# First chunk's values and third unit's queries and keys as seven block products

## The chip, the cores and the metric

The kernel runs on one core of a Trainium2 chip. The core has five engines with a queue of instructions each: TensorE (PE in the profile, with its weight loads as PEld), VectorE (DVE), ScalarE (ACT), GpSimd (POOL) and SyncE (SP), which here only issues DMAs. The time is the device time of one execution in microseconds; the time before is the median of three runs.

## The reference

One layer: a layer norm, causal attention with 32 heads of 16, and a gate, over x of shape 2 x 1024 x 512 in float32.

```python
xn = _layernorm(x, axis=-1)
s = _L0_attn_ref(xn, Wq, bq, Wk, bk, Wv, bv, Wo, bo)       # causal, 32 heads of 16
g = _silu(_L0_ffn_ref(xn, W_base, b_base, W_gate, A, B))   # 8 experts of rank 16, top 2
x = x + s * g
```

Inside the attention, q, k and v are xn @ W.T + b. The scores are q . k / 4 under a causal mask, then softmax, then the sum over v, then the output projection.

## The kernel before

**Work and stages.** Each batch (2) is cut into two chunks of 512 tokens, and the 512 columns of queries and keys into four groups `oc` of 8 heads. A *unit* (b, oc, c) is the attention of one chunk's queries for one group. The units run in the order of `units` (lines 1305 to 1311): the first is (0, 0, 0), the second (0, 1, 0), the third (0, 0, 1), which is the second chunk of the first group. A unit is a list of *steps*. `plan` strings the steps of all units together (144), and the loop at the end of `direct` does for each step n: `scores(n)` (PE into two PSUM tiles, then two exponentials on ScalarE), `values(n - 1)` (PE, the weights of the step before times the values), `masked(n)` (GpSimd clears what lies above the diagonal), and `fill(n)`, which puts other work in. The first unit has steps 0 to 4, the second 5 to 9, the third 10 to 22.

**Who sets the order.** The whole program is written down in one pass, and each engine takes its instructions in that order. `fill` (line 1513) is a planner: a `Task` is a generator with a due step, a cost in PE time (`MM` = 0.853) and conditions. It takes PE tasks until the step's share is spent, and then lets through what waits in the list `later`: small pieces for the other engines, each with the step from which it may go. A piece with an entry in `costs` goes when ScalarE is reckoned calm, and at the latest at its second number. `Metered` and `Queue` keep the planner's reckoned times of VectorE, ScalarE and SP.

**Buffers.** Projections write PSUM tiles of the tag `mm`, of which there are two, so a product can only begin when the product before the last one has been read. Scores have two tiles a step (`ps_s`, two of each name), so scores n + 1 can begin when the exponentials of step n have read theirs. The exponentials' results `pt` have three buffers.

**Products by blocks.** Most projections are made by a scheme in which a 2 x 2 block matrix product takes seven block products instead of eight: `four_sums` makes four sums t1 to t4 of weight blocks, `sums_task` four sums s0 to s3 of token blocks, and the products p1, p2, p6, p7, p5, p3, p4 (for queries and keys q1 to q4, with the query's and the key's columns as the two block columns) are added up on VectorE. Value and gate products are `block_task`, those of queries and keys `qk_blocks_task`. Weight sums are stored to DRAM (`kept`) and loaded again piece by piece into four buffers with the tag `wp` (`issue_parts`). Three projections are made in the plain way: the first unit's queries and keys (`first_task`), the second and third unit's (`qk_task`), and the first chunk's values (`v_task`, one of four token tiles at a time, each 4 groups of four matmuls).

**Rounding.** From the second unit on, keys and queries are split into a high part in fp32r and a remainder. `split_keys` rounds the keys on ScalarE (`kT<-kf`) and takes the remainder on VectorE; `split_queries` and `copy_remainder` do so for queries; `place_keys` and `place_queries` put the remainders onto other partitions, by two DMAs each on SP's queue. The first unit uses unrounded keys `kf_0_0_0`; they are also the first keys of the third unit, so they are shuffled, rounded and placed later (`apart` in `first_task`). `pair_up` is a copy on ScalarE that rearranges a weight tile's columns before a block product or `qk_task` can use it.

Almost all vector and scalar instructions are recorded at line 56 and all SP DMAs at line 72, so the profile's groups are told apart by their tiles.

Of the kernel before, what the change touches and what calls it, by code (L numbers as in the profile page):

```python
# [18 lines left out]
P = 128  # L19
D = 512  # L20
# [77 lines left out]
def direct(ctx, tc, sound, x, wq, wk, wv, wo, wb, wa, wg, wB, bq, bk, bv, bo, bb, out):  # L98
# [259 lines left out]
    def first_task():  # L358
# [78 lines left out]
        later.append((0, lambda: pair_up(wqks[1])))  # L437
        paired = lambda: pair_up(wqks[0])
        costs[paired], costs[apart] = (1.1, 5), (1.1, 6)
        later.append((3, paired))  # L440
        later.append((4, apart))
        yield 2 * MM
# [117 lines left out]

    first_v = []

    def v_task(b, i):
        if not first_v:
            first_v.append(value_tile(b, 0))
        pv = mm_tile("pv")
        for _ in project(pv, b, i, wv_sb):
            yield MM
        ve.tensor_add(
            heads(first_v[0])[:, i, :, 0:HD],  # L570
            pv.rearrange("p (h r) -> p h r", h=H),
            bv_sb.rearrange("p (h r) -> p h r", h=H),
        )
        vs[b, i] = first_v[0][:, i]
        yield MM

# [4 lines left out]
    groups = (  # L584
        [("v", 0, 1), ("qk", 0, 1, 1)],
        [("gate", 0, 0), ("qk", 0, 0, 2), ("qk", 0, 0, 3)],
# [29 lines left out]

    def combine_task(name, given=None):

        src, bias = weights[name]
        w = given or load_whole(src, f"w_{name}", later)  # L620
        for _ in range(0 if given else 6):
            yield WAIT
        at = {
            (i, j): w[:, 2 * i : 2 * i + 2, BK * j : BK * j + BK]
            for i in range(2) for j in range(2)
        }
        yield from four_sums(at, {int(t[1]): at[p] for t, p in IN_PLACE.items()})
        kept = dram.tile([P, KC, D], F32, tag=f"kept_{name}", bufs=1, name="kept")
        ve.tensor_tensor(bias[:, BK:D], bias[:, BK:D], bias[:, 0:BK], ALU.subtract)
        yield WAIT  # L630
        combined[name] = kept
        if given:
            sp.dma_start(out=kept, in_=w)
            kept_at[name], kept_lands[name] = now[0], sp.landing()
        if name == "gate":
            first = stages.index(("gate", 0, 0))
            for j, part in enumerate(PARTS):
                if part in IN_PLACE:
                    places[first, j] = at[IN_PLACE[part]]
                    held.add((first, j))  # L640
        for kc in range(0 if given else KC):
            yield WAIT
            sp.dma_start(out=kept[:, kc], in_=w[:, kc])
            kept_at[name], kept_lands[name] = now[0] + KC - 1 - kc, sp.landing()
        yield WAIT
        if given:
            yield WAIT
        while name == "gate" and made[first] < len(PARTS):
            yield WAIT

    def issue_parts():
        while issued[0] < len(parts):
            k, j = parts[issued[0]]
# [22 lines left out]
            issued[0] += 1  # L676

    def qk_weights_task(n):

# [4 lines left out]
        else:  # L684
            if n >= 2:
                wqks.append(load_qk(oc))
                for _ in range(3):
                    yield WAIT
                paired = lambda: pair_up(wqks[n])
                costs[paired] = (1.05, now[0] + 4)  # L690
                later.append((now[0] + 1, paired))
                while any(x[1] is paired for x in later):
                    yield WAIT
                yield WAIT
            w = wqks[n]
            yield from four_sums(
                {(i, j): w[:, 4 * j + 2 * i : 4 * j + 2 * i + 2] for i in range(2) for j in range(2)},
                {t: w[:, 2 * KC + 2 * t - 2 : 2 * KC + 2 * t] for t in range(1, 5)},
            )
            qk_kept[oc] = dram.tile([P, 4 * KC, P], F32, tag=f"kept_qk{oc}", bufs=1, name="kept")  # L700
            qk_ready[n] = now[0]
            for i in range(4):
# [127 lines left out]

    def qk_blocks_task(k):

        _, b, c, oc = stages[k]
        at, w = tokens(k), wqks[b * KC + oc]
        qk_begun.append((b, oc, c))
# [3 lines left out]
        less, bias = b_less[:, oc : oc + 1], b_pair[:, KC + oc : KC + oc + 1]  # L839
        place = {"11": 0, "21": 2, "12": 4, "22": 6, "t1": 8, "t2": 10, "t3": 12, "t4": 14}  # L840

        def product(name, a):
            ps = mm_tile(name)[:, 0:BK]
            n = place[PARTS[made[k]]]
            for kc in range(2):
                matmul(ps, lhsT=w[:, n + kc], rhs=a[:, kc], start=kc == 0, stop=kc == 1)
            made[k] += 1
            return ps
# [8 lines left out]
        yield MM  # L857
        s = yield from sums_of(k)
        add(keys[0], product("q6", s[1]), keys[0])
# [6 lines left out]
        yield MM  # L866
        add(keys[0], product("q3", s[3]), keys[0])
        yield MM
        add(q[1], product("q4", at(1, 1)), q[1], less)
        splits.append((now[0] + 1, lambda: split(b, oc, c, qf, kf), (b, oc, c)))  # L870
        qk_done[b, oc, c] = now[0]
        ended[0] += 1
        yield MM

    def values_task(k):
# [511 lines left out]
    for b in range(NB):  # L1387
        for c in range(NC):
# [11 lines left out]
            for oc in range(KC):  # L1400
                takes = {"acc": 1}
                if (b, oc, c) in units[1:3]:
                    Task(
                        starts[b, oc, c] - (1 if c else 2), qk_task(b, oc, c), 8 * MM, takes=takes | {"qT": 1, "kT": 1}, uses=xn, frees=takes,
                        ready=lambda u=units[units.index((b, oc, c)) - 1], t=turned_: u in qk_begun
                        and t() and (u == units[0] or now[0] >= starts[units[1]]),
                    )
                elif oc or b or c:
                    stage(
# [3 lines left out]
            if not b and not c:  # L1413
                room["v"] -= 1
                for t in range(TT):
                    Task(
                        s0 + (1, 2.9, 5, 2.9)[t], v_task(b, t), 4 * MM, uses=xn + [("xnT", "wv")],
                        ready=turned_,
                    )
                Task(  # L1420
                    3, combine_task("v", wv_sb), 0.0, after=5, uses=[("xnT", "wv")],
                )
                for n, name in enumerate(("gate", "out")):
                    Task(
                        (20, 48)[n], combine_task(name), 0.0, after=(9, 34)[n], takes={"xnT": 1},
                        frees={"xnT": 1}, ready=lambda n=n: len(combined) > n,
                    )
                for n in range(2 * KC):
                    Task(
                        (20, 13, 24, 28)[n] if n < KC else -9, qk_weights_task(n), 0.0, after=9,  # L1430
                        ready=lambda n=n: n < 2 or (
# [771 lines left out]
```

## Time and profile before

| what | us |
|---|---|
| median of three runs | 548.98 (548.91 to 549.15) |
| the profiled execution, its own time | 548.63 |
| its span, first to last instruction | 546.8 |
| PE busy in the span | 536.9 |
| DVE, ACT, POOL busy | 333.0, 351.7, 117.9 |
| first value product begins | 17.64 |
| scores of step 10 begin (third unit) | 67.76 |

Times in a timeline are microseconds from the span's start, followed by the length; `xN` is the number of instructions in a piece, and a bracket says how long the engine sat idle before it and what ended that. A float32 matmul leaves two records. `pv` are the first chunk's values, `pq` and `pk` queries and keys made in the plain way, `p` and `q` block products, `ph` the routing's logits, `s` scores, `av` values times weights. The ends of matmuls are modelled, so a busy PE may hold short waits.

### The profile page before, as it was taken

How to read it: one execution, taken by the hardware profiler on the slowest of the kernel's cores; microseconds unless marked ns; L12 is line 12 of the kernel's file. 1: busy time of each engine (PE TensorE's matmuls, PEld its weight loads, DVE VectorE, ACT ScalarE, POOL GpSimd, SP SyncE). 2: the span in 40 equal slices, each digit the busy share in tenths (PEclk: the TensorE clock that was granted, in tenths of full speed). 3: DMA queues.
4: the chain of work that ended last, by engine and by line, in shares of the span. 5: the costliest groups of instructions: out<-in, count | busy, mean ns of one | idle time of the engine just before them, and what ended most of it. 6: DMA issues, size and time to landing. Idle time of an engine off the chain costs nothing.

```text
span 546.8 us, 19460 instructions
## 1 busy us (share of the span) xinstructions
PE 536.9 (98%) x8411; PEld 278.3 (51%) x8411; DVE 333.0 (61%) x692; ACT 351.7 (64%) x390; POOL 117.9 (22%) x249
## 2 busy tenths in 40 slices
PE   8999999999999999999999999999999999999994
PEld 8435444554455544454645554454545554455562
DVE  4435586665575975576379766575176553648842
ACT  2437754776776867657667756657668767777531
POOL 2213401020134411030123321130123331020500
PEclk9999999999999999999999999999999999999999
DMA  8734357356527376813646545640123221652301
GB/s 262 183 101 159 133 161 233 99 177 197 175 99 230 120 243 209 220 42 100 199 153 197 187 131 176 198 137 23 64 99 123 86 75 46 232 172 86 99 22 66
DMA packets 66798, 78.11 MB, mean 143 GB/s; under 512 B 9880, under 2 KB 51872, under 8 KB 66064
## 3 DMA queue, kind: packets, MB, share of 16 engines
q1 hardware_dynamic: 66688, 76.78, 44.1%
q8 instruction: 68, 1.11, 0.8%
q14 instruction: 26, 0.21, 0.1%
q10 hardware_dynamic: 16, 0.00, 0.0%
HBM read 45.34 MB, written 19.37 MB: 118 GB/s over the span
## 4 chain that ended last, share of the span: by engine, by line
PE 95%; DVE 2%; ACT 1%; issue 0%; POOL 0%; ACTq 0%; POOLq 0%; DVEq 0%
PE av L1676 26%; PE p L257 23%; PE s L1624 18%; PE q L257 14%; PE ph L257 3%; PE pv L257 3%; PE po L257 2%; PE pk L257 1%; PE pq L257 1%; ACT pt L56 1%; PE warm L212 1%; PE pq_first L385 1%; PE h L257 1%; DVE g L56 1%; PE pk_first L385 1%
## 5 line engine op out<-in xcount | busy, mean ns | idle before, releaser
L56 ACT ACTIVATE pt<-s 128x1024 f32<-128x1024 f32 x288 | 290.4, 1025 | 151.8 <-PE s L1624 144.8
L1652 POOL TENSOR_SCALAR_AFFINE_SELECT pt<-pt 128x256 f32<-128x256 f32 (+1 forms) x224 | 108.6, 501 | 405.4 <-ACT pt L56 404.8
L1676 PE MATMUL av<-pt,v 128*32 128x512 f32 (+3 forms) x1680 | 155.7, 467 | 0.4 <-DVE v L56 0.2
L1624 PE MATMUL s<-qT,kT 32*128 32x512 f32 (+3 forms) x1616 | 108.2, 363 | 0.7 <-ACT pt L56 0.5
L1624 PEld LDWEIGHTS s<-qT,kT 32*128 32x128 f32 x1616 | 62.0, 183 | 59.4 <-issue 34.9
L1676 PEld LDWEIGHTS av<-pt,v 128*32 128x32 f32 x1680 | 41.1, 108 | 54.6 <-issue 38.8
L257 PE MATMUL p<-wt,asum 128*32 128x256 f32 x864 | 52.6, 379 | 0.0
L257 PE MATMUL q<-asum,wqk 128*32 128x256 f32 x832 | 51.1, 379 | 0.0
L257 PEld LDWEIGHTS p<-wt,asum 128*32 128x32 f32 x864 | 28.5, 110 | 26.4 <-issue 11.2
L257 PE MATMUL q<-xnT,wqk 128*32 128x256 f32 x624 | 39.5, 379 | 0.0
L257 PEld LDWEIGHTS q<-asum,wqk 128*32 128x32 f32 x832 | 26.8, 110 | 23.7 <-issue 7.2
L56 DVE TENSOR_TENSOR g<-p,g 128x512 f32<-128x512 f32 x20 | 13.8, 690 | 26.6 <-PE p L257 26.5
L257 PEld LDWEIGHTS q<-xnT,wqk 128*32 128x32 f32 x624 | 20.2, 110 | 18.5 <-issue 6.6
L56 DVE SCALAR_TENSOR_TENSOR kf<-q,kf 128x256 f32<-128x256 f32 x39 | 16.5, 424 | 21.3 <-PE q L257 20.6
L257 PE MATMUL p<-w,xnT 128*32 128x256 f32 x448 | 27.4, 379 | 0.0
L257 PE MATMUL p<-w,asum 128*32 128x256 f32 x320 | 20.8, 379 | 0.0
L257 PEld LDWEIGHTS p<-w,xnT 128*32 128x32 f32 x448 | 14.9, 110 | 10.6 <-issue 3.3
L257 PEld LDWEIGHTS ph<-wag_sb,xnT 128*32 128x32 f32 x512 | 15.3, 110 | 3.9 <-issue 3.0
L257 PE MATMUL ph<-wag_sb,xnT 128*32 128x136 f32 x512 | 16.6, 279 | 0.0
L56 DVE TENSOR_TENSOR x<-p,x 128x512 f32<-128x512 f32 x15 | 10.3, 688 | 10.3 <-PE p L257 10.2
L257 PE MATMUL po<-wo,oT 128*32 128x512 f32 x128 | 16.5, 592 | 0.0
L56 DVE TENSOR_TENSOR qT<-qf,qT 128x512 fp32r<-128x512 f32 x15 | 10.4, 696 | 9.4 <-ACT qT L56 9.4
(150 smaller groups left out, 565.8 us busy)
## 6 DMA issues: line engine op xcount, KB each, us to landing
wt<-kept SPq DMA_DIRECT2D x36, 256.0 KB
qT<-qT SPq DMA_DIRECT2D x30, 256.0 KB
x<-in_x_dram SPq DMA_DIRECT2D x16, 256.0 KB
kept<-wqk SPq DMA_DIRECT2D x16, 256.0 KB
wqk<-kept SPq DMA_DIRECT2D x4, 1024.0 KB
kT<-kf SPq DMA_DIRECT2D x30, 128.0 KB
scr<-sq SPq DMA_DIRECT2D x6, 512.0 KB
xnT<-scr SPq DMA_DIRECT2D x24, 128.0 KB
```

What stands on the lines that cost most here:

```text
L56: return getattr(self.engine, name)(*args, **named)
L212: nc.tensor.matmul(warm[:, n % 4 * P : n % 4 * P + P], lhsT=ident, rhs=ident, start=True, stop=True)
L257: nc.tensor.matmul(o[j : j + 32], lhsT=lhsT[:, j : j + 32] if len(lhsT.shape) == 2 else lhsT[:, j // 32], rhs=rhs, start=start, stop=stop,)
L385: nc.tensor.matmul(ps[:, cols], lhsT=w[:, k, :], rhs=xnT[:, k, cols], start=k == 0, stop=k == KC - 1)
L1624: nc.tensor.matmul(ss[s // 2][:, s % 2, col : col + w], lhsT=keys[rows, kt % TT * P : kt % TT * P + P], rhs=q[rows, halves * par + half_, ...
L1652: nc.gpsimd.affine_select(out=d, in_=d, compare_op=ALU.is_ge, fill=0.0, base=0, pattern=[[0, d.shape[1]], [1, P]], channel_multiplier=-1,)
L1676: nc.tensor.matmul(avs_now[par][32 * s : 32 * s + 32, q0 : q0 + w], lhsT=vs[b, kt][:, h * VS - HD * par : h * VS - HD * par + HP], rhs=pt[ ...
```

## The change

1. The first chunk's values are made by `early_task` as seven block products instead of four plain tiles. It makes its eight sums itself, on VectorE: six before the first product's addition, two before the second's. Its products are written in the order p1, p2, p6, p7, p4, p5, p3, with each addition written right behind its product. The weight sums lie in the four `wp` buffers and not in place, and `keep_task` stores them to DRAM by four DMAs; the products of the second chunk's values can be loaded only after that.
2. The third unit's queries and keys become a block stage: seven products of two groups of four matmuls at 256 columns. Their token sums s0 to s3 are shared with the second chunk's values. In this unit the keys are rounded right behind the product q3, and the queries behind q4, instead of by the planner's `splits`.
3. For that, the first weights' pairing copy (`paired`) is offered at step 1 and the weight sums of the first group follow at step 3.
4. The first unit's keys (`apart`) are offered at step 7 instead of 4, and at the latest at 8 instead of 6.
5. Due steps of some tasks change (second unit's `qk_task` 3, gate weights 18).

The diff, cut to its core:

```diff
@@ first_task
-        paired = lambda: pair_up(wqks[0])
-        costs[paired], costs[apart] = (1.1, 5), (1.1, 6)
-        later.append((3, paired))
-        later.append((4, apart))
+        def paired():
+            pair_up(wqks[0])
+            paired_at.append(now[0])
+
+        costs[paired], costs[apart] = (1.1, 4), (1.1, 8)
+        later.append((1, paired))
+        later.append((7, apart))
...
-        [("v", 0, 1), ("qk", 0, 1, 1)],
+        [("qk", 0, 1, 0), ("v", 0, 1), ("qk", 0, 1, 1)],
...
+    def keep_task():
+        kept = dram.tile([P, KC, D], F32, tag="kept_v", bufs=1, name="kept")
+        for part, (r, o) in IN_PLACE.items():
+            sp.dma_start(
+                out=kept[:, 2 * r : 2 * r + 2, BK * o : BK * o + BK], in_=early_sums[part]
+            )
+            if part in ("t3", "t2"):
+                yield WAIT
+        combined["v"], kept_at["v"], kept_lands["v"] = kept, now[0], sp.landing()
...
@@ qk_blocks (was qk_blocks_task)
+        soon = (b, oc, c) == units[2]
...
         add(keys[0], product("q3", s[3]), keys[0])
+        if soon:
+            qT, kT = split_tiles(b, oc, c)
+            split_keys(kT, kf, kf)
+            later.append((now[0], lambda: place_keys(kT, kf)))
         yield MM
         add(q[1], product("q4", at(1, 1)), q[1], less)
-        splits.append((now[0] + 1, lambda: split(b, oc, c, qf, kf), (b, oc, c)))
+        if soon:
+            split_queries(qT, qf)
+
+            def remainder():
+                copy_remainder(qT)
+                urgent.append((now[0], lambda: place_queries(qT)))
+
+            later.append((now[0] + 1, remainder))
+            room["acc"] += 1
+        else:
+            splits.append((now[0] + 1, lambda: split(b, oc, c, qf, kf), (b, oc, c)))
...
+    def early_task():
+        x0 = xnTs[0, 0]
+        at = lambda i, j: x0[:, 2 * j : 2 * j + 2, BK * i : BK * i + BK]
+        raw = {
+            (i, j): wv_sb[:, 2 * i : 2 * i + 2, BK * j : BK * j + BK]
+            for i in range(2) for j in range(2)
+        }
...
+        def product(name, a, w):
+            ps = mm_tile(name)
+            for i in range(2):
+                for kc in range(2):
+                    matmul(
+                        ps[:, i * BK : i * BK + BK],
+                        lhsT=a[:, kc, i * P : i * P + P],
+                        rhs=w[:, kc],
+                        start=i + kc == 0,
+                        stop=i + kc == 2,
+                    )
+                    yield MM / 2
+            return ps
+
+        sub = lambda o, a, b: ve.tensor_tensor(o, a, b, ALU.subtract)
+        sub(t[1], raw[0, 1], raw[0, 0])
+        sub(s[2], at(0, 0), at(1, 0))
+        sub(s[1], at(1, 1), s[2])
+        sub(t[2], raw[1, 1], t[1])
+        ve.tensor_tensor(s[0], s[1], at(0, 0), ALU.add)
+        sub(t[3], raw[1, 1], raw[0, 1])
+        p1 = yield from product("p1", at(0, 0), raw[0, 0])
+        add(s12, p1, bias(0))
+        sub(t[4], raw[1, 0], t[2])
+        sub(s[3], at(0, 1), s[1])
+        p2 = yield from product("p2", at(0, 1), raw[1, 0])
+        add(s11, p2, s12)
+        begin_with[0].due = 2
+        sub(bv_sb[:, BK:D], bv_sb[:, BK:D], bv_sb[:, 0:BK])
+        p6 = yield from product("p6", s[1], t[2])
+        add(s12, p6, s12)
+        p7 = yield from product("p7", s[2], t[3])
+        add(s21, p7, s12)
+        ve.tensor_tensor(s22, s21, bias(1), ALU.add)
+        p4 = yield from product("p4", at(1, 1), t[4])
+        add(s21, p4, s21)
+        begin_with[0].due = 3
+        p5 = yield from product("p5", s[0], t[1])
+        add(s12, p5, s12)
+        add(s22, p5, s22)
+        ve.tensor_tensor(s12, s12, bias(1), ALU.add)
+        p3 = yield from product("p3", s[3], raw[1, 1])
+        add(s12, p3, s12)
...
-                if (b, oc, c) in units[1:3]:
+                if (b, oc, c) == units[1]:
+                    begin_with.append(Task(
+                        1, early_task(), 14 * MM, takes={"v": 1},
+                        uses=xn + [("xnT", "wv")], ready=turned_,
+                    ))
                     Task(
-                        starts[b, oc, c] - (1 if c else 2), qk_task(b, oc, c), 8 * MM, takes=takes | {"qT": 1, "kT": 1}, uses=xn, frees=takes,
...
+                        3, qk_task(b, oc, c), 8 * MM, takes=takes | {"qT": 1, "kT": 1}, uses=xn, frees=takes,
                     )
+                elif (b, oc, c) == units[2]:
+                    stage(
+                        qk_blocks_task, ("qk", b, c, oc), starts[b, oc, c] - 2, 7 * MM,
+                        takes | {"qT": 1, "kT": 1}, xn,
+                        lambda t=turned_: t() and begin_with[0] not in tasks,
+                    )
+                    summed[0].due = 4
...
-                for t in range(TT):
-                    Task(
-                        s0 + (1, 2.9, 5, 2.9)[t], v_task(b, t), 4 * MM, uses=xn + [("xnT", "wv")],
-                        ready=turned_,
-                    )
-                Task(
-                    3, combine_task("v", wv_sb), 0.0, after=5, uses=[("xnT", "wv")],
-                )
+                Task(4, keep_task(), 0.0, after=4, ready=lambda: begin_with[0] not in tasks)
```

## The prediction

> **What bounds the kernel now.** I read the page first, then the chain of work that ended last piece by piece over the first 120 us, then the instructions in order of time on every engine, and last the order in which the changed program's instructions stand on each engine. The page's busy times, then its chain:
>
> ```profile
> PE 536.9 (98%) x8411; PEld 278.3 (51%) x8411; DVE 333.0 (61%) x692; ACT 351.7 (64%) x390; POOL 117.9 (22%) x249
> ...
> PE 95%; DVE 2%; ACT 1%; issue 0%; POOL 0%; ACTq 0%; POOLq 0%; DVEq 0%
> ```
>
> PE sets the time: PE work removed is time won, and every wait of PE is time lost unless a later wait gets shorter. The chain around the change (start us, length, what; a matmul leaves two records):
>
> ```profile
> 27.14 5.15 PE pv L257 x48
> 32.29 3.43 PE pq L257 x32
> 35.73 3.43 PE pk L257 x32
> 39.16 1.08 PE s L1624 x16
> 40.24 1.00 PE av L1676 x16
> ...
> 46.82 0.70 DVE v L56
> 47.52 0.14 issue
> 47.66 1.07 PE av L1676 x16
> ...
> 66.10 1.73 PE p L257 x32
> ...
> 71.22 0.67 PE s L1624 x5
> ```
>
> The reader is to see that pieces follow each other without a gap, except for the last value tile (46.82 to 47.66). A group of four strips costs 3.43/4 = 0.858 us at 512 columns and 1.73/4 = 0.43 at 256. A plan step outside its filler costs scores 1.08 (first unit) or 0.67 to 0.73, plus av 1.00. I number steps by their scores; step 10 is the third unit's first (scores at 67.83 now).
>
> Durations that the sums below use, from the timeline:
>
> ```profile
> 25.28 0.17 DVE L56 TENSOR_SCALAR rstd<-mv 128x4 f32<-128x4 f32 x1
> 39.95 1.06 ACT L56 ACTIVATE kT<-kf 128x1024 fp32r<-128x1024 f32 x1
> 41.04 0.69 DVE L56 TENSOR_TENSOR kf<-kf,kT 128x512 f32<-128x512 f32 x1 [2.75 <-ACT kT L56]
> 52.77 0.76 DVE L56 STREAM_SHUFFLE low<-kf 128x512 f32<-128x512 f32 x1
> 61.01 1.92 ACT L56 ACTIVATE pt<-s 128x1024 f32<-128x1024 f32 x2
> 62.82 0.63 ACT L56 ACTIVATE qT<-qT 128x512 fp32r<-128x512 f32 x1
> 63.47 1.11 SPq L72 DMA_DIRECT2D qT<-qT  x2
> 68.39 0.54 SPq L72 DMA_DIRECT2D wt<-kept  x1
> 90.89 0.42 DVE L56 SCALAR_TENSOR_TENSOR kf<-q,kf 128x256 f32<-128x256 f32 x1 [0.38 <-PE q L257]
> ```
>
> **Which part can differ.** From step 22 on, PE's instructions stand in the same order in both programs, apart from four matmuls moved by one step near the end (steps 137 and 138). So the difference is what PE gains or loses up to step 22, carried to the end. I walk PE from 17.71, where values begin in both.
>
> **Removed.** Values: 4 x 4 groups of 0.858 = 13.7 become 7 x 4 of 0.43 = 12.1: -1.6. Third unit: 8 groups, 6.9, become 14 of 0.43, 6.1: -0.8. The gap at 46.82 goes, but scores of 0.67 stood inside it: -0.2. Together -2.6. The copy that pairs the first weights (1.15 on ScalarE) moves from step 4 to step 1, where ScalarE is idle from 24.5 to 26.2: nothing. The routing's logits move to steps 3 to 5, at the same PE cost. Two value-weight loads leave SP's queue at step 1, four 256 KB stores enter at step 5 behind the second transposed half; nothing waits for them before step 8. If that cover went, their 4 x 0.5 us of issue would delay the products of step 8.
>
> **Added, steps 0 to 3: VectorE.** It is free at 15.54, and the value weights have landed (the DMA that waits for their semaphore issues at 13.62). In front of the first product's addition stand six 128x512 sums. Such sums take 0.69 (0.77 and 0.89 where GpSimd works beside them); I take 0.72, as the four weight sums at 49.56 take 2.95 together. So 15.54 + 4.3 = 19.9; p1's addition to 20.55; t4 and s3 to 22.0; p2's addition to 22.7. PE: p1 to 19.4, p2 21.15, a quarter of p6 21.6, scores 22.65, av 23.7 (0.05 behind p2's addition), rest of p6 25.0, p7 26.7. Then p4 needs p6's PSUM buffer (two buffers), and in front of p6's addition stand 0.4 for the bias and next chunk's statistics, 21.96 to 25.45 now = 3.5: 22.7 + 0.4 + 3.5 + 0.7 = 27.35. **Stall 0.65.** Likewise pq needs p5's buffer; normalizing (2.1) and transposes (1.4) stand in front of p5's two additions: 29.8 + 3.5 + 1.4 = 34.8 against 34.6. **Stall 0.2.** pk ends 41.65. All sums at 0.69 halve these 0.9; at 0.85 they are 2.
>
> **Steps 3 to 6: ScalarE.** Steps 3 to 5 get shorter (1.08 + 1.00 + 6 x 0.23 = 3.5; step 5 only 0.67 + 1.00 + 0.93 = 2.6), while ScalarE does kf 0.69, kT 1.06 and 2.0 of exponentials after pk, and a 0.27 copy per logits tile. Exponential 3 ends at 45.4, scores 4 wants its buffers at 45.1 to 45.2; scores 6 waits for exponential 5. **Stalls 0.35 and 0.25.** Step 7 begins at 55.2. The second transposed half, now about 2.5 later than its last issue end of 48.8 and landing some 1.6 after it, is there at 52.9, before q2 at 54.3.
>
> **Step 7: five q products in a row.** VectorE: q2's addition to 55.65, four token sums of 0.69 to 58.4, two routing operations to 58.85, only then q6's addition (59.3). q6 waits 0.15 for its sum; q5 needs q6's buffer: 0.55; q4 0.05. **Stall 0.75.** q3 ends at 61.1, q4 at 62.0; q3's addition ends at 61.55.
>
> **Steps 8 and 9: who is queued behind whom.** In the built order ScalarE has kT, qT and the routing exponential in front of exponential 8, and VectorE has the remainder of the keys (which waits for kT) in front of q4's addition (which qT waits for). So after 61.55: kT 1.06, remainder 0.69, q4's addition 0.42, qT 1.06, routing 0.22, with 0.05 each between: exponential 8 runs from 65.2 to 67.2, though its scores are there at 62.75. Now no such pair stands there with a VectorE round trip inside it. PE does av 7 and the value product p1 until 65.5; scores 9 need both buffers of exponential 8: done at 67.85 where 66.15 was possible. av 8 waits for its masks, 0.84 later: **stall 1.7 + 0.2.** p2 ends at 70.8.
>
> **Step 10: the first unit's keys.** They are rounded only now. VectorE: query remainder to 65.7, six small routing operations (1.3 alone, 1.9 beside GpSimd as at 67.03: 1.6), p1's addition 0.68, shuffle 0.76: 68.75. ScalarE: rounding 1.06, query copy 0.63: 70.5. SP's queue: two query placements 1.1 and a weight load 0.54, then the first half of the keys is issued at 72.2. Now that placement (issued 67.19) finds the DMA engines busy from 68.2 to 69.4 for its two halves, so the first lands about 1.6 after issue: 73.8. Scores 10 need it; PE comes at 70.8: **stall 3.05** (landing 1.4 to 2.2, small operations as above: 2.3 to 4.2). Before, these keys were placed at 56.15, eleven us early. And were they there at once, scores 10 would still wait for exponential 9, behind that copy, to 72.5: 1.7.
>
> End of step 10: 73.85 + 0.67 + 1.0 + 1.73 = 77.25, with p6 done; now the same work ends at 71.22 + 1.73 = 72.95: **+4.3**. Step by step: -2.6 + 0.9 + 0.6 + 0.75 + 1.9 + 3.05 = +4.6; the seams between chain pieces make up the rest, and I take the walk. In step 15 a finished unit's normalization (five operations behind q2's addition, 3.4 in all) stands in front of q6's addition: q5 waits **0.5**. After it the queues have room; the swap near the end I put at 0 (between -0.3 and +0.3). **Sum +4.8 to +5.1, taken as +4.9.**
>
> The profiled execution took 548.63 us, its span 546.8 and 1.8 around it; the walk is made in that span, and gives 551.7 + 1.8 = 553.5. On the median of 548.98, 0.35 higher, it is 553.9.
>
> **A rule against the change.** The granted clock is 9 tenths or more in every slice, and 0.998 on the mean: nothing here shows what a wait of 3 us does. The Trainium skill, "TensorE: Matmul & The Clock Gate", section "What's actually happening", says that an idle window of some 3.4 us puts PE's clock to half, and that it takes a busy window of that length to come back. A stall of 3.05 does not fill a free-running window; one of 4.2 could. By the row nothing is added; by the rule up to 3.4 us at half speed, an estimate of 1.7: 555.6. I follow the row, since the stall is below the window.
>
> **Rivals.** (1) The clock gate as above: 555.6. For it: two stalls with 3 us between them; against it: the length. (2) VectorE bounds steps 0 to 3: GpSimd masks beside the six sums cost 0.85 each, 1.1 more: 555.0. For it the 0.89 row; against it that most sums show 0.69. (3) The chain behind q3 is covered: if its exponential and the keys come by the time PE does (the point is keys landed by 70.8, not 73.8, and exponential 8 done by 65.5), the 4.95 us at steps 9 and 10 go, and the change ends at 549.0, no change; with the smaller stalls also less than I think, down to 546.4. For it, that 98% busy now leaves no such wait anywhere; against it, each engine takes its queue in order. That the seven products don't shorten PE is excluded by counts: 28 groups of 0.43 for 16 of 0.858.
>
> **Numbers.** My walk 0.63, with its own range 552.0 to 556.0 (early stalls 0.4 to 2, step 10 2.3 to 4.2); the gate 0.10; VectorE 0.09; covered 0.18, of which faster 0.07, same 0.06, slower 0.05. A measurement can tell 0.2% (1.1 us) from no change. So faster 0.07, same 0.06, slower 0.87. The range 550.0 to 556.5 leaves out most of the covered case and the far end of the gate.
>
> **What would show it.** Right: PE idle before scores 10 for about 3 us, ended by the key placement; exponential 8 starting some 2.4 us after its scores; VectorE's addition before p4; step 22 about 4.9 later than 113.2. Wrong: scores 10 starting by 71, or PE's pieces without gaps through steps 7 to 10, or a granted clock under 9 tenths about 75 us.

## The result, and the profile after

The changed kernel takes **557.46 us** (median of 5 runs, 556.08 to 557.80), the kernel before 548.98 beside it (548.76 to 549.47): the ratio is 1.0147, with a 95% interval of 1.0134 to 1.016, or 8.5 us more. The direction was forecast, the size was not: 553.9 was said, and 557.46 lies above the upper end of the range, 556.5. The profiled execution of the changed kernel is the shortest of the five, 556.08 us with a span of 554.3, so the traces compare 554.3 with 546.8: 7.5 us. Its mean granted clock is 0.995; the three longest runs show 0.990. The part on why the prediction failed comes back to that difference.

The lines of the page, of the changed kernel:

```profile
PE 538.2 (97%) x8555; PEld 284.5 (51%) x8555; DVE 342.6 (62%) x709; ACT 351.1 (63%) x389; POOL 117.9 (21%) x249
...
PEclk9999989999999999999999999999999999999999
...
PE 92%; DVE 4%; ACT 2%; issue 1%; DMA 1%; POOL 0%; DVEq 0%; ACTq 0%; POOLq 0%
```

PE's share of the chain fell from 95 to 92%, and one slice of the clock's row, the one that holds 69 to 83 us, went from 9 to 8: a granted clock under 9 tenths at about 75 us, which the prediction had named as a sign of being wrong. The chain of the changed kernel around that slice (start us, length, what):

```profile
60.88 0.43 DVE kf L56
61.33 1.07 ACT kT L56
62.40 0.02 issue
62.42 0.69 DVE kf L56
63.12 0.41 DVE qf L56
63.55 1.07 ACT qT L56
...
67.32 0.76 DVE low L56
68.10 1.07 ACT kT L56
69.17 0.02 issue
69.19 0.69 DVE low L56
...
71.55 2.85 DMA kT<-low
74.39 0.14 issue
74.53 1.23 PE s L1731 x8
75.75 1.86 PE av L1783 x16
77.62 1.77 PE p L257 x32
```

This is the chain that the prediction wrote down, round trip for round trip: the third key product's addition ends at 61.3 (61.55 forecast), the keys' rounding, their remainder, q4's addition and the queries' rounding follow, and then the first unit's keys. Two things differ. The placement takes 2.85 us from its issue on SP to landing, where 1.6 was forecast. And what follows it is slow: eight strips of scores take 1.23 us, for which step 12 needs 0.67, and the value products 1.86 instead of 1.0.

Adding up each step's scores, value products and filler in both traces, against the same work without a wait, gives this account:

| place | forecast, us | measured, us |
|---|---|---|
| values begin later, in front of all that changed | 0 | 0.1 |
| work removed | -2.6 | -2.5 (what is left when the rest is taken from the sum) |
| VectorE in steps 0 to 3 | 0.9 | 0 |
| ScalarE in front of scores 4 and 6 | 0.6 | 0.6 |
| step 7 | 0.75 | 1.2 |
| steps 8 and 9 | 1.9 | 1.5 |
| wait for the first keys, step 10 | 3.05 | 4.29 |
| half clock behind that wait | 0 | 1.4 |
| step 15 | 0.5 | 0.5 |
| **shift at step 22** | **+4.9** | **+7.1** |

The forecast terms add up to 5.1; the prediction took its walk from piece to piece, 4.9. The work removed is a remainder in this account, but the chain shows most of it directly: the value products take 12.2 us of PE where they took 13.9.

From step 22 on the distance stays the same up to step 137, moves back and forth around steps 138 to 140, where four matmuls changed their step, and is 7.0 at the last scores and at the last addition. The other 0.5 us of the 7.5 lie behind that addition, in the last stores. They take 4.9 to 5.9 us in the thirteen traces of this case, 5.0 and 5.5 in these two, so nothing ties this part to the change.

### The profile page after: what moved, and what is told of

The parts are those of the page before. It is cut to its first block, busy times and chain, and to the rows that moved or that the text cites. A ratio compares the mean times of both kernels' runs of the same rounds, so it can differ in the third digit from the quotient of the medians.

```text
span 554.3 us, 19779 instructions
## 1 busy us (share of the span) xinstructions
PE 538.2 (97%) x8555; PEld 284.5 (51%) x8555; DVE 342.6 (62%) x709; ACT 351.1 (63%) x389; POOL 117.9 (21%) x249
## 4 chain that ended last, share of the span: by engine, by line
PE 92%; DVE 4%; ACT 2%; issue 1%; DMA 1%; POOL 0%; DVEq 0%; ACTq 0%; POOLq 0%
PE av L1783 25%; PE p L257 25%; PE s L1731 18%; PE q L257 14%; PE ph L257 3%; PE po L257 2%; ACT pt L56 1%; PE warm L212 1%; DVE g L56 1%; PE pq_first L385 1%; PE h L257 1%; PE pq L257 1%; PE pk L257 1%; DVE key L56 1%; PE pk_first L385 1%
## 5 line engine op out<-in xcount | busy, mean ns | idle before, releaser
L257 PE MATMUL p<-wt,asum 128*32 128x256 f32 x960 | 58.6, 379 | 0.0
L257 PE MATMUL q<-asum,wqk 128*32 128x256 f32 x896 | 55.2, 379 | 0.7 <-DVE kf L56 0.4
L257 PEld LDWEIGHTS p<-wt,asum 128*32 128x32 f32 x960 | 31.7, 111 | 29.2 <-issue 11.9
L257 PE MATMUL q<-xnT,wqk 128*32 128x256 f32 x672 | 42.8, 379 | 0.1
L257 PEld LDWEIGHTS q<-asum,wqk 128*32 128x32 f32 x896 | 28.9, 110 | 27.4 <-issue 7.2
L257 PEld LDWEIGHTS q<-xnT,wqk 128*32 128x32 f32 x672 | 21.6, 110 | 19.8 <-issue 6.4
L56 DVE TENSOR_TENSOR v<-p,v 128x512 f32<-128x512 f32 x22 | 15.0, 688 | 14.6 <-PE p L257 14.3
L56 ACT ACTIVATE kT<-kf 128x1024 fp32r<-128x1024 f32 x15 | 15.8, 1053 | 3.8 <-DVE kf L56 3.7
L56 DVE COPY oT<-av 128x512 f32<-128x512 f32 x15 | 10.3, 684 | 11.6 <-PE av L1783 11.6
L56 DVE TENSOR_TENSOR kf<-kf,kT 128x512 f32<-128x512 f32 x15 | 10.3, 684 | 11.6 <-ACT kT L56 11.6
```

Of the source, the lines that this page charges most:

```text
L56: return getattr(self.engine, name)(*args, **named)
L257: nc.tensor.matmul(o[j : j + 32], lhsT=lhsT[:, j : j + 32] if len(lhsT.shape) == 2 else lhsT[:, j // 32], rhs=rhs, start=start, stop=stop,)
```

## Experiments

**The first keys put back early.** In the changed kernel only, the keys' rounding is offered at step 4 and lands at step 5:

```diff
-        costs[paired], costs[apart] = (1.1, 4), (1.1, 8)
+        costs[paired], costs[apart] = (1.1, 4), (1.1, 4)
...
-        later.append((7, apart))
+        later.append((4, apart))
```

> The changed kernel, with one thing put back: the first unit's keys are rounded and placed at step 5 instead of step 9. Theory A, the late keys hold up step 10: the 4.3 us wait for their placement goes; scores 10 then waits only for the queries' placement, whose copy no longer stands behind the rounding of the keys (0.5 to 1.0 us left), and with no long wait the granted clock stays above 0.9 from 74 to 78 us, which gives back the 1.4 us that scores 10 and the value products behind it took too long. Sum -3.3 to -3.8 and -1.4 to -2.8: 551.5 to 552.5 us. Theory B, the chain behind the third unit's last key product holds step 10 up just as long, and the keys only happened to land last: the wait becomes one for the queries' placement of 3 us or more, 555 us or more.

Measured: 550.72 us (550.20 to 551.47), ratio 1.0029 (1.0017 to 1.0042). That is 6.7 us less than the changed kernel, and 0.8 less than theory A's lower end. Scores 10 do not wait at all. From the instructions in order of time on PE:

```profile
70.06 0.74 PE L1731 MATMUL s<-qT,kT 32*128 32x512 f32 x8
```

Theory A had left 0.5 to 1.0 for the queries' placement; but with the keys' rounding out of the way, the queries' copy ran at 66.3 instead of 69.1, their placement was issued at 67.0 and had landed when PE came. Theory B falls. Late keys are thus 6.7 of the 8.5 us (6.5 by the two ratios, each against the kernel before on its own chip).

**Late keys alone.** The same two numbers changed the other way, in the kernel before:

```diff
-        costs[paired], costs[apart] = (1.1, 5), (1.1, 6)
+        costs[paired], costs[apart] = (1.1, 5), (1.1, 8)
...
-        later.append((4, apart))
+        later.append((7, apart))
```

> The kernel before, with one thing of the change: the first keys are rounded at step 9, behind the third unit's own keys. Theory A: the rounding (1.06) stands in front of exponential 9 and waits for a shuffle behind the third unit's remainder, the placement is issued near 69.8 us and lands 1.6 to 2.9 us later, at 71.4 to 72.6, where scores 10 starts at 67.83 now: a wait of 3.5 to 4.8 us, and from about 3.4 us on the half clock behind it, 1.4 us more. 552.5 to 555 us, 553.5 the likeliest. Theory B, the late keys cost only together with the third unit's block products: 550 us or less, no drop of the clock.

Measured: 554.72 us (554.66 to 555.81), ratio 1.0102 (1.0085 to 1.0119). Theory A gives the place and the size; neither the early sums nor the block products are needed for the loss. PE in order of time, then the busy time in three stretches (the length, the busy us of PE, PEld, DVE, ACT and POOL, each with its instructions in brackets, then the granted clock, the DMA share and GB/s):

```profile
72.00 1.23 PE L1624 MATMUL s<-qT,kT 32*128 32x512 f32 x8 [3.86 <-DMA kT<-low]
```

```profile
68.08:71.49 3.41, 0.06 (x4) 0.00 (x0) 2.12 (x9) 3.00 (x4) 0.96 (x2) 1.00 0.31 115
71.49:74.90 3.41, 2.90 (x28) 1.36 (x32) 2.28 (x5) 1.02 (x1) 0.66 (x3) 0.50 0.39 120
74.91:78.32 3.41, 3.41 (x36) 1.34 (x28) 0.78 (x2) 1.02 (x1) 0.00 (x0) 0.50 0.00 0
```

The wait is 3.86 us, and then the clock stands at exactly one half for twice 3.4 us. In this execution (the longest of the four) scores 11 begin 7.3 us later than in the kernel before, and the clock is 3.0 of that: scores 10 and what follows up to scores 11 take 6.41 us instead of 3.39.

**The clock: the wait filled with matmuls.** Four matmuls of the first unit's weights on the first chunk's tokens go to the scores' buffer, in the place where PE only waits:

```diff
         ss = [ps_s.tile([P, 2, C], F32, tag="s", name=f"s{p}") for p in range(2)]
+        if n == 10:
+            for k in range(KC):
+                nc.tensor.matmul(
+                    ss[0][:, 0], lhsT=wqks[0][:, k, :], rhs=xnTs[0, 0][:, k, :],
+                    start=True, stop=True,
+                )
```

> The changed kernel, with four matmuls of 128x512 (0.86 us each by the page's rows, 3.43 together) written to the first scores buffer ahead of scores 10, which overwrite it; they do no work for the output, and stand where PE only waits. Theory A, idleness of PE drops the clock: PE is busy from about 70.8 to 74.2, the keys land as before at 74.4, but the granted clock stays above 0.9; scores 10 take 0.7 instead of 1.23 and the value products 1.0 instead of 1.86. 1.4 us less than the changed kernel where one stretch of half clock was paid, 2.8 where two were: 554.7 to 556 us. Theory B, the clock falls for another cause (the transfers' load, say): scores 10 slow as before, 557.5 us.

Measured: 555.27 us (555.08 to 555.39), ratio 1.0112 (1.0095 to 1.0129). Four more matmuls make the changed kernel 2.2 us shorter (1.9 by the two ratios). PE in order of time, and two stretches:

```profile
71.34 3.70 PE L1723 MATMUL s<-xnT,wqk 128*128 128x512 f32 x8 [0.39 <-ACT pt L56]
75.23 0.74 PE L1737 MATMUL s<-qT,kT 32*128 32x512 f32 x8 [0.20 <-DMA kT<-low]
```

```profile
74.00:76.00 2.00, 1.80 (x15) 0.62 (x17) 0.00 (x0) 0.00 (x0) 0.00 (x0) 1.00 0.88 247
76.00:78.00 2.00, 2.00 (x40) 1.23 (x44) 1.29 (x2) 1.92 (x2) 0.00 (x0) 1.00 0.04 12
```

The keys again land 2.85 us after their issue and the transfer engines are as busy (0.88), but the clock stays at 1.00: PE's idleness drops it, not the transfers. All four runs lie within 0.4 us of each other.

**How long a wait it takes.** The same with one matmul (`range(1)`), so that PE idles in two pieces, and then with two (`range(2)`):

> As the kernel whose wait was filled with four matmuls, but with one of them (0.86 us): PE then idles some 2.9 us instead of 4.3 before the keys land, which they do at the same time. It asks whether a wait as long as the one that the prediction forecast (3.05) drops the clock. Theory A, the granted clock falls only when PE has idled for the better part of 3.4 us or more: clock above 0.9 from 74 to 80 us, and the same time as with four matmuls, 555.3 us (554.8 to 555.8). Theory B, 3 us are enough: scores 10 and what follows at half speed as in the changed kernel, 556.5 to 558 us.

> As the kernels whose wait was filled with four matmuls (no half clock) and with one (half clock for 6.8 us, although PE idled only 0.4 and 2.6 us), but with two: PE idles 0.4 and then some 1.75 us. Theory A, the gate weighs PE's busy share in stretches of 3.4 us that run on their own, and halves the clock where that share is under about a half: whether it falls here depends on where the stretch begins; some runs at 554.9 to 555.4 us and some 1.5 to 2 us longer. Theory B, it takes one unbroken wait of 2.5 us or more: all runs at 554.9 to 555.4 us, clock 1.00 throughout.

Measured: with one, 557.04 us (556.72 to 557.12), ratio 1.0149 (1.0134 to 1.0165); with two, 555.62 us, the four runs at 554.48, 555.09, 556.15 and 556.58, ratio 1.0111 (1.0095 to 1.0126). With one, theory B was right: the half clock comes back in full although PE now waits only 2.60 us in one piece. With two, the times are as A said: two runs are about 1.6 us longer than the other two. One matmul, PE and stretches of 3.4 us:

```profile
70.70 1.12 PE L1723 MATMUL s<-xnT,wqk 128*128 128x512 f32 x2 [0.40 <-ACT pt L56]
74.43 1.23 PE L1737 MATMUL s<-qT,kT 32*128 32x512 f32 x8 [2.60 <-DMA kT<-low]
```

```profile
69.80:73.20 3.40, 1.63 (x11) 0.32 (x3) 3.06 (x13) 1.76 (x2) 1.27 (x2) 1.00 0.64 230
73.20:76.60 3.40, 2.17 (x20) 1.09 (x24) 0.00 (x0) 0.83 (x1) 0.00 (x0) 0.50 0.48 155
76.60:80.00 3.40, 3.40 (x40) 1.56 (x36) 1.38 (x2) 1.22 (x2) 0.00 (x0) 0.50 0.02 5
```

Two matmuls, in the profiled execution (the longest of the four):

```profile
72.80:76.20 3.40, 1.49 (x21) 0.71 (x24) 0.72 (x2) 0.37 (x1) 0.00 (x0) 1.00 0.72 222
76.20:79.60 3.40, 3.40 (x40) 1.73 (x36) 1.38 (x2) 1.68 (x2) 0.00 (x0) 0.50 0.02 5
```

And the changed kernel:

```profile
70.80:74.20 3.40, 0.00 (x0) 0.00 (x0) 2.14 (x8) 0.70 (x1) 1.13 (x2) 1.00 0.94 308
74.20:77.60 3.40, 3.07 (x28) 1.52 (x32) 0.69 (x1) 1.02 (x1) 0.00 (x0) 0.50 0.28 82
77.60:81.00 3.40, 3.40 (x55) 1.44 (x48) 2.19 (x5) 1.87 (x2) 0.00 (x0) 1.00 0.10 31
```

Row after row: a stretch in which PE was busy 0.00, 0.06, 1.63 or 1.49 of 3.4 us is followed by half clock. Half clock went on for a second stretch when PE had been busy 2.17 or 2.90 of the first, and ended after one when it had been busy 3.07 or 3.40. The stretches lie on a fixed grid. In the trace of the changed kernel the granted clock changes at 5.91, 74.17, 77.59 and 552.04 us, that is 20, 21 and 160 times 3.413 us after the first change; in each of the other twelve traces, too, all changes lie on such a grid, and where it begins differs from trace to trace. So the clock changes in steps of 3.4 us, which agrees with the window of 3.41 us in the Trainium skill, "TensorE: Matmul & The Clock Gate", section "What's actually happening"; but where the page speaks of an idle window, windows with PE busy 44 and 48% were enough here. The measurement decides. What counts is how much of a wait falls into one stretch, and the kernel does not set where the stretches begin: with two matmuls the drop came 3.1 us after PE had stopped, with one matmul 1.4 us after. That can give one program run times 2 us apart. Only one execution of each kernel was traced, so for the other runs it is argued, not shown.

**A shorter wait.** In the changed kernel, one weight load on SP is held back behind the keys' placement, by returning early from the function that issues them:

```diff
     def issue_parts():
-        if "v" not in combined:
+        if "v" not in combined or now[0] in (8, 9):
             return
```

> The changed kernel with one weight load (256 KB, for the product p5 of step 12) issued behind the first keys' placement instead of in front of it. Theory A, the placement landed 2.85 us after its issue, not 1.6 as forecast, because that load and the queries' placement lay in the transfer engines in front of it: issue 0.6 us earlier, landing in 2.0 to 2.4, so PE waits 2.9 to 3.3 us instead of 4.3, and at that length the clock mostly stays up. 1.0 to 1.4 for the wait and 1.4 to 2.8 for the clock: 553 to 555 us. Theory B, the queries' placement alone makes it slow: 2.85 us from issue as before, a wait of 3.7, half clock still: 556.5 us or more.

Measured: 554.65 us (553.17, 554.26, 555.04, 555.74), ratio 1.0114 (1.0099 to 1.013). SP's queue, the chain and PE in order of time:

```profile
70.93 1.19 SPq L72 DMA_DIRECT2D kT<-low  x2
```

```profile
70.93 2.03 DMA kT<-low
```

```profile
73.10 0.74 PE L1731 MATMUL s<-qT,kT 32*128 32x512 f32 x8 [2.83 <-DMA kT<-low]
```

Issue is 0.6 earlier, and the placement lands 2.03 us after it instead of 2.85: the 256 KB in front of it had cost both, as A said. The wait is 2.83 us, shorter than the prediction's 3.05. The profiled execution, 553.17, keeps a clock of 1.00 through it. Its grid, counted from its first change of the clock at 6.62 us, shows how: a boundary at 71.48 cuts the wait in two.

```profile
68.06:71.47 3.41, 2.22 (x44) 1.34 (x36) 2.08 (x9) 3.35 (x4) 0.63 (x1) 1.00 0.35 131
71.48:74.89 3.41, 1.79 (x31) 1.02 (x34) 1.96 (x7) 0.98 (x2) 0.64 (x1) 1.00 0.75 265
```

So a stretch with PE busy 52% (1.79 of 3.41 us) kept the clock up, where 48% (1.63 of 3.40) had let it fall, and a wait of 2.83 us cost nothing behind it, where one of 1.91 had cost a stretch of half clock. The other three runs, at a mean clock of 0.993 to 0.996, are 1.1 to 2.6 us longer. So A was right on the wait and only partly on the clock, "mostly stays up": their times suggest that it mostly did not, but none of them was traced.

**The early values alone.** Keys at step 5, and the third unit by whole products again:

```diff
-        [("qk", 0, 1, 0), ("v", 0, 1), ("qk", 0, 1, 1)],
+        [("v", 0, 1), ("qk", 0, 1, 1)],
...
                 elif (b, oc, c) == units[2]:
-                    stage(
-                        qk_blocks_task, ("qk", b, c, oc), starts[b, oc, c] - 2, 7 * MM,
-                        takes | {"qT": 1, "kT": 1}, xn,
-                        lambda t=turned_: t() and begin_with[0] not in tasks,
+                    Task(
+                        starts[b, oc, c] - 2, qk_task(b, oc, c), 8 * MM, takes=takes | {"qT": 1, "kT": 1}, uses=xn, frees=takes,
+                        ready=lambda t=turned_: t() and begin_with[0] not in tasks,
                     )
-                    summed[0].due = 4
```

> The changed kernel with the first keys at step 5 and the third unit's queries and keys computed by whole products as before: what is left of the change is the first chunk's values by seven block products, their sums made early. Theory A, these gain what the counts say: -1.6 for the products and -0.2 for the gap before the last value tile, with VectorE's stalls at 0 to 0.3 as the changed kernel's trace has them: 547.2 to 548 us. Rival, VectorE bounds steps 0 to 3 or the earlier routing logits cost ScalarE time in steps 3 to 6: 549.5 us or more.

Measured: 549.33 us (548.64 to 550.45, 20 runs), ratio 1.0005 (0.9998 to 1.0012). The time lies between theory A's and the rival's. The 1.8 us are won, and lost again in three places that theory A had left out; the first two are on ScalarE in steps 3 to 6, where the rival looked: scores 4 take 1.38 instead of 1.07, scores 6 take 1.31 instead of 0.67 (half of it because exponential 5 stands behind the keys' rounding at step 5), and in step 10 a product waits for its weights, whose loads are queued behind the third unit's key placement on SP:

```profile
71.49 1.93 PE L257 MATMUL p<-wt,asum 128*32 128x256 f32 x32 [0.76 <-DMA wt<-kept]
```

**Both parts, with those waits taken out.** The first keys are rounded as the last thing of the early values, in step 2, where VectorE and ScalarE have nothing to do, and two weight loads of step 10 are issued at step 6. One kernel has the whole change, the other is the one above, with whole products for the third unit:

```diff
-        costs[paired], costs[apart] = (1.1, 4), (1.1, 8)
+        costs[paired] = (1.1, 4)
...
-        later.append((7, apart))
+        begin_with.append(apart)
...
-            if part[0] == "t" and now[0] < kept_at.get(name, now[0]) + 1:
+            if part[0] == "t" and now[0] < kept_at.get(name, now[0] + 1) + (name != "v"):
...
-            if part[0] == "t" and kept_lands[name] > clock[0] + 1.0 and now[0] < kept_at[name] + 3:
+            if part[0] == "t" and kept_lands[name] > clock[0] + 1.0 and now[0] < kept_at[name] + (0 if name == "v" else 3):
...
         add(s12, p3, s12)
+        begin_with[1]()
```

> The whole change, with the first keys rounded at the end of the early values (step 2), where ScalarE and VectorE have nothing to do, and with two weight loads of step 10 issued at step 6. Against the kernel with the keys at step 5 (550.7 us) exponential 5 no longer stands behind the rounding: scores 6 take 0.98 instead of 1.32. 550.4 us (549.9 to 550.9). What stays of the loss is then the third unit's block products: waits of 1.2 in step 7 and 1.15 in step 9 against 0.84 saved. Were these waits not the cause, the kernel would come out at or below the kernel before: 548.5 us or less.

> The values by block products with early sums, the third unit by whole products as before, the first keys rounded at the end of the early values (step 2), two weight loads of step 10 issued at step 6. Against the kernel with the early values alone (549.3 us): scores 6 0.33 shorter, and the 0.76 us that p6 of step 10 waited for its weights gone: 548.2 us (547.6 to 548.8), at or just below the kernel before. Rival, the waits only move (the loads delay the denominators' transfer behind them on SP's queue, say): 549.2 us or more. The difference to the kernel with both parts is the price of the third unit's block products: 2.2 us by the waits counted there.

Measured: the whole change 550.50 us (550.31 to 550.98), ratio 1.0034 (1.0021 to 1.0047); values alone 548.99 us (548.40 to 549.57, 13 runs), ratio 0.9998 (0.999 to 1.0006). Scores 6 take 0.97 in both, and p6's wait is gone. The second kernel is 0.7 to 1.1 us ahead of the one before from step 22 to step 138 of its trace and gives 0.5 back at the seam there, which the expectation did not allow for. The difference of the two, 1.5 us (2.2 forecast), is the price of the third unit's block products: 0.8 us fewer matmuls, bought with waits of 1.2 in step 7 and 1.4 in steps 8 and 9 in that trace.

**The third unit's rounding behind exponential 8.** In the kernel with the whole change and early keys:

```diff
-            split_keys(kT, kf, kf)
-            later.append((now[0], lambda: place_keys(kT, kf)))
+            def rounded():
+                split_keys(kT, kf, kf)
+                place_keys(kT, kf)
+
+            later.append((now[0] + 1, rounded))
...
-            split_queries(qT, qf)
-
             def remainder():
+                split_queries(qT, qf)
                 copy_remainder(qT)
```

> The whole change with the keys rounded at step 2 (550.5 us), and the third unit's own rounding (keys and queries) behind exponential 8 instead of in front of it. Theory A, the rounding pair in front of exponential 8 makes scores 9 wait: that wait (1.15 us) goes, and 0.7 to 1.5 us of it come back at step 10, where scores wait for exponential 9 and for the queries' placement, now both later: 549.8 to 550.8 us, 550.3 the likeliest, the wait moved from step 9 to step 10. Theory B, scores 9 wait for something else: the wait stays at step 9, and the placement's lateness comes on top, 551 us or more.

Measured: 551.21 us (550.87 to 551.50), ratio 1.0038 (1.0024 to 1.0051). That is above A's range, but by the ratios only 0.2 us more than the kernel it starts from (1.0034), which the intervals do not tell apart. The wait moved as A said (scores 9 take 0.67 instead of 1.58), and nothing was won by it: from scores 8 to scores 11 the trace shows 12.0 us instead of 11.6.

```profile
71.30 0.74 PE L1734 MATMUL s<-qT,kT 32*128 32x512 f32 x8 [1.69 <-DMA qT<-qT]
```

The queries' placement is now issued at 68.9. Here the chain from the last product to a placement that has landed is longer than the time to step 10; where ScalarE's part of it stands only chooses which step waits.

**ScalarE relieved in steps 3 to 6.** In the kernel with the early values and whole products:

```diff
-        if c:
+        if True:
             act.activation(
                 kT, pk.unsqueeze(1).to_broadcast([P, 2, C]), AF.Identity, bias=bias_k
             )
...
-            act.copy(hl[:, t], ph)
+            (act.copy if b or c else ve.tensor_copy)(hl[:, t], ph)
```

> The early values, whole products for the third unit, keys rounded at step 2 (549.0 us, as before the change), and two things taken off ScalarE in steps 3 to 6: the second unit's keys are rounded straight from PSUM, as a later chunk's are, with VectorE taking the copy of 0.69, and the routing logits of the first chunk are copied by VectorE. Scores 4 and scores 6 each wait 0.31 us for an exponential behind those operations; both waits go: 548.4 us (548.0 to 548.9). Rival, VectorE gets late with the sums or copies behind it, and the time stays at 549.0 or goes above.

Measured: 548.49 us (547.39 to 549.73, 18 runs), ratio 0.999 (0.9983 to 0.9998): 0.5 us below the kernel before, the one version here that beats it, by less than the 0.2% named in the prediction. Scores 4 are back at 1.07; scores 6 stay at 0.97, so ScalarE's logits copies were not what they wait for. Step 5 is only 2.6 us long, and exponential 5 alone takes 2.

## Why the prediction was right or wrong

The place of the loss and the chain behind it were right. Two terms of the sum failed: the landing of the first keys' placement, put at 1.6 us and measured at 2.85, and the clock behind the wait, put at 0 and measured at 1.4 us in the profiled execution. Term by term:

- **The counts of PE's work** agree with the account: -2.6 forecast, -2.5 left over here, and -2.6 left over in the kernel with the keys at step 5.
- **VectorE's stalls in steps 0 to 3** (0.65 and 0.2) did not come. The terms mis-sized are the sums' and additions' 0.65 to 0.72: rows of 0.69 follow each other every 0.60 us, since one record overlaps the next (p1's addition begins at 19.76, the three behind it at 20.37, 20.97 and 21.57). p6's addition ended at 26.58, not 27.35, and p4 could start at once. Rival 2 falls with this, though two sums did take 0.9.
- **ScalarE in steps 3 to 6**: 0.35 and 0.25 forecast, 0.31 and 0.31 measured.
- **Step 7**: 0.75 forecast, 1.2 measured. The waits stand where they were said to stand, for the token sum and for q6's addition. The brackets count less than the loss, because a record's end overlaps the next start by some 0.2 us; from start to start, q6 comes 0.48 us late (0.15 forecast), q5 0.38 more (0.55) and q4 0.32 more (0.05):

```profile
56.77 1.93 PE L257 MATMUL q<-asum,wqk 128*32 128x256 f32 x32 [0.29 <-DVE asum L56]
58.87 1.93 PE L257 MATMUL q<-asum,wqk 128*32 128x256 f32 x32 [0.17 <-DVE kf L56]
```

- **Steps 8 and 9**: the order on ScalarE was right to 0.6 us, and exponential 8 began at 64.6 (65.2 forecast); 1.9 forecast, 1.5 measured.
- **Step 10**: the mechanism was right, the size was not. Of the sum's terms, the issue came 0.65 earlier than forecast (71.55) and PE 0.55 earlier (70.24), which cancel by luck; the landing, "about 1.6 after issue", was 2.85. It had been read from a placement that shared the engines with little: they were busy 23% of its 1.6 us (67.19 to 68.79 in the kernel before), and 89% of these 2.85 us. Here queries, weights and keys were issued one behind the other, SP in order of time:

```profile
69.71 1.11 SPq L72 DMA_DIRECT2D qT<-qT  x2
70.92 0.53 SPq L72 DMA_DIRECT2D wt<-kept  x1
71.55 1.10 SPq L72 DMA_DIRECT2D kT<-low  x2
```

- **The clock** was the step that failed in its reasoning: "I follow the row, since the stall is below the window". The row showed no wait of this length at all, so it could not speak against the rule; and the premise is wrong too, as waits of 2.60 and 1.91 us halved the clock: a wait need not fill a window. With the landing as it was, the wait of 4.29 us did fill one (PE busy 0.00 from 70.8 to 74.2). So rival 1 was not an alternative to the main case but a part of it. Its own term, 1.7 us, is of about the right size: 1.4 in the profiled execution. The three runs with a mean clock of 0.990 are 1.4 to 1.7 us longer than the profiled one; one more stretch of 3.4 us at half speed would make 1.7. No trace of them was taken, so that this is where they lost it is argued, not shown; the two kernels that were profiled at 0.990 show two stretches. Nor does the mean clock alone tell it: the four runs with one matmul in the wait, at 0.990 to 0.995, lie within 0.4 us.
- **Step 15**: 0.5 forecast, 0.5 measured.

So 4.9 became 7.1 in the trace by the landing (+1.25), the clock (+1.4) and step 7 (+0.45), less what VectorE and ScalarE did not cost (-0.9 and -0.4), with 0.4 left over. That two terms were too high hid part of the miss, which is luck. The rest of the 8.5 us is 0.5 in the last stores and 1.0 by which the median stands further above the profiled execution than in the kernel before, perhaps by the clock of the longer runs. Rival 3, the chain that is covered, came out wrong: the point that it named, keys landed by 70.8, was missed by 3.6 us.

## What to carry to other kernels

When a stage that PE waits on moves late, price what follows the wait as well as the wait. In the traced executions, counted up to the next scores, a wait of 4.29 us cost 1.4 us of half clock behind it, one of 3.86 cost 3.0, one of 2.60 cost 2.6, one of 1.91 cost 1.7, and one of 2.83 nothing: the length of the wait alone does not give the price, since it depends on how the wait falls on stretches that the kernel does not set. Read a transfer's landing from a case with the same transfers queued in front of it. And before work is put early or late, look for the stretch where the engines it needs are all free: the rounding cost 5.6 to 6.7 us at step 9, 0.3 at step 5 and nothing visible at step 2.

## What was not expected of the hardware

The clock falls to exactly one half for one or two whole stretches of 3.4 us, after a stretch in which PE was busy 48% or less. It needs no empty stretch, and what brings it back is more than what keeps it up: PE busy for 64 or 85% of a stretch at half clock was not enough, 90% was. A stretch with PE busy 52% kept the clock up, so in these traces the border lies near one half; it is known no more closely than that, as PE's busy time is taken from records whose ends are modelled. Four matmuls whose result is not used, in front of the late operand, took about 2 us off the time.
